# Gathering neighbours on quarters of the matrix array, in sixteen chunks of 64 columns

## The chip, the cores and the metric

The kernel runs on one core of a Trainium2 chip. The core has a matrix engine (TensorE, "PE" in the profile, with its weight loads apart as "PEld"), a vector engine (VectorE, "DVE"), a scalar engine (ScalarE, "ACT"), a general engine (GpSimd, "POOL") and SyncE ("SP"), which here issues all DMAs. Each engine works through its own list in order and waits on semaphores for the others. The metric is the device time of one execution, in microseconds (us); lower is better.

## The reference

Two graph layers over 16 graphs of 1024 nodes with 64 features. About 8 in 1000 entries of the adjacency are set, apart from the diagonal, which is always set. Layer 0 is attention with 8 heads over the neighbours, layer 1 additive attention with one head; each is followed by a residual sum and a layer normalisation.

```python
# layer 0, per graph
scores = einsum('bmhd,bnhd->bhmn', q, k) * scale + edge_bias[edges]
scores = where(edges > 0, leaky_relu(scores, 0.2), -1e9)
x = layernorm(x + einsum('bhmn,bnhd->bmhd', softmax(scores), v) @ Wp + bp)
# layer 1, per graph
e = einsum('bijf,f->bij', leaky_relu(u[:, :, None] + v[:, None], 0.2), a)
e = where(adj > 0, e, -9e15)
x = layernorm(x + elu(einsum('bij,bjf->bif', softmax(e), hp)))
```

## The kernel before

**Lists in place of a dense matrix.** The rows of a graph are taken in groups of eight (128 groups). For each group the kernel lists the columns in which any of the eight rows has a neighbour, and gathers those columns of x once for all eight. A second, dense version (`all_pairs`) stands behind a flag and runs only if some list overflows. A group has 120 slots: two halves of 56 (`CAP2`) and the eight rows themselves.

**Making the lists (`prepare`).** Per graph the adjacency is loaded, reduced with a matmul to one number per group and column (`pat`, L347; how many rows have it and which), and turned into keys (L353) that hold that number and the column. The columns stand in four segments of 256. VectorE takes the largest keys of a segment eight at a time (`max`, L359 and L392) and strikes them out (`match_replace`, L360 and L394), five rounds in all. Between the first and the second round, L367 to L385 split columns that several rows share into one key per row (`MULT` = 4). A segment gives 34 slots (`WIN`); two neighbouring segments share the 12 middle ones of a half, the second filled from its far end (L402, L403). The columns of the slots go to DRAM (`col_d`, L412), the row codes too (`slot_d`, L424), and come back spread over the partitions as `rows_s` (16 DMAs, L431), from which `finish` makes the mask. `prepare` is a generator of 41 pieces.

**Gathering.** 128 rows make 8 tiles of 16 groups. For each tile and layer, `load` (L482) spreads the tile's column list `col_d` over all partitions as `cb`; `indicate` (L494) compares it with the partition's own number, twice (`jrow`, once for each 128 columns of a segment), which gives the 0/1 matrix `f`; `gather` (L518) multiplies x, split exactly into three bf16 parts (`t3`, made by `thirds` on GpSimd), with `f`. Its matmuls contract over all 128 partitions and write 64 of the 128 output partitions each; one half of the slots (`hs`) is 26 matmuls, most with 272 columns, into one PSUM bank, and ScalarE copies it to `xg` (L524).

**Around it.** Layer 0: `queries` (L623) makes q for the tile; `score` (L644) multiplies it with `xg` and adds the mask; VectorE adds a constant (`sc`, L652) and makes the leaky relu and the row maximum (L660, L661); `exps` (ScalarE, L670), `divide` (VectorE's reciprocal L677 and GpSimd's product L678), `turn` and `turn_weights` (transposes L537 and L686), `attend` (L696), `heads` (L712) and `rows` (L728). Layer 1: `own_rows` (L771 on GpSimd), `project` (L779, L785, then relu L791 and sum L792), `weigh` (L806), `exps`, `turn_weights` (L820, copied to `eT` by ScalarE, L822), `attend` (L831), `rows` (L289).

**Order of the work.** All of it is written out by hand, with every engine's list in program order. The main loop makes one step per tile: in step g layer 0 gathers tile g, scores tile g-1 and finishes g-2 and g-3, while layer 1 does the same for tile u = g - 12. So 12 steps have layer 0 alone, 116 both layers and 12 layer 1 alone, and a few close the pipeline. At five places in a step (`lists.place`) pieces of the next graph's `prepare` are put in, by a quota per step (`QUOTA`), and one piece of GpSimd and normalisation work from two side lists.

**Buffers that set an order.** In PSUM, tag "g" has two banks (gather halves, layer 1's transposes, `pa`), "s" two (score, `po`, `pz`), "p" two (queries, transposes), "e" one: `back`, `pe` of `weigh` and `pt1` of layer 1's `turn_weights` take turns in it. In SBUF `cb` has three buffers, `f` four, of which a tile uses two.

## Time and profile before

| What | Value |
|---|---|
| median of 3 runs | 2473.73 us (2468.94 to 2477.21) |
| the profiled execution, span | 2474.2 us |
| TensorE busy | 2230.1 us (90%), 46658 matmuls |
| VectorE busy | 1858.2 us (75%) |
| ScalarE busy | 1602.8 us (65%) |
| GpSimd busy | 1227.3 us (50%) |
| DMA queue of the kernel | 29.7% of 16 engines' span, 231.85 MB |
| first `score` starts, last one | 85.5 us, 2319.7 us |
| one batch (8 steps) in the middle | 144 to 147 us |

A group line reads: line, engine, operation, output<-inputs, size, x how often | busy time in us, mean ns of one | idle time of the engine just before them in us, and what ended most of it. Matmuls are pipelined: the mean of one is from its start to its end, and several are under way at once, so busy time, not count times mean, is what they cost. A timeline line reads: start in us, duration in us, engine, line, operation, and how many were merged into it. A line of busy times by stretch reads: stretch, its length, busy time of each engine with the number of its instructions, the granted share of TensorE's clock, the DMA engines' share and GB/s.

### The profile page before, as it was taken

The page shows a single profiled execution, that of the slowest core. Times are in us where ns is not written, and L with a number is a line of the kernel's source. Part 1 is how long each engine was busy: PE and PEld are TensorE (multiplying, and loading weights), DVE is VectorE, ACT ScalarE, POOL GpSimd, SP SyncE. Part 2 cuts the span into 40 slices and gives each one's busy share as a digit, 9 for nine tenths or more (in the row PEclk, how much of TensorE's full clock was granted, in tenths as well). Part 3 has the DMA queues.
Part 4 walks back from the last instruction along what each step waited for, and adds up shares of the span by engine and source line. Part 5 has one row for each costly group of instructions (what it writes and reads, how often), then busy time and mean ns, then how long its engine had stood idle before and what let it go on. Part 6 is the DMA issues. An engine that isn't in the chain of part 4 may idle for free. (4 is left out here: it accounts for less than half of the span.)

```text
span 2474.2 us, 107346 instructions
## 1 busy us (share of the span) xinstructions
PE 2230.1 (90%) x46658; PEld 1852.8 (75%) x46658; DVE 1858.2 (75%) x4591; ACT 1602.8 (65%) x5585; POOL 1227.3 (50%) x1570
## 2 busy tenths in 40 slices
PE   4577999999999999999999999999999999999995
PEld 3466877777787777778777777787777788788763
DVE  5587888787878878787787878778787877866532
ACT  2255766767677676767667676776767667677753
POOL 1133545545464555546456454545645555555552
PEclk9688999999999999999999999999999999999998
DMA  3422422423333242333224233232423323132110
GB/s 104 133 63 87 134 102 80 142 78 112 110 97 104 74 148 78 117 105 104 97 73 149 78 105 117 91 109 73 150 79 105 103 93 113 58 101 75 52 47 21
DMA packets 192691, 238.78 MB, mean 97 GB/s; under 512 B 91732, under 2 KB 157332, under 8 KB 192212
## 3 DMA queue, kind: packets, MB, share of 16 engines
q1 hardware_dynamic: 192212, 231.85, 29.7%
q8 instruction: 368, 6.03, 1.0%
q14 instruction: 111, 0.91, 0.1%
HBM read 226.58 MB, written 5.21 MB: 94 GB/s over the span
## 5 line engine op out<-in xcount | busy, mean ns | idle before, releaser
L518 PE MATMUL pg<-f,x 128*64 128x272 bf16 (+2 forms) x13312 | 822.5, 276 | 43.5 <-DVE f L494 28.7
L518 PEld LDWEIGHTS <-x 128*64 128x64 bf16 x13312 | 675.0, 111 | 158.6 <-issue 125.8
L678 POOL TENSOR_TENSOR ls<-ls,den 128x480 f32<-128x480 f32 x256 | 294.7, 1151 | 677.7 <-DVE den L677 677.0
L494 DVE TENSOR_SCALAR f<-cb,jrow 128x2176 bf16<-128x2176 bf16 x512 | 457.9, 935 | 11.4 <-DMA cb<-col_d 11.4
L524 ACT COPY xg<-pg 128x448 f32<-128x448 f32 x512 | 267.5, 525 | 299.8 <-PE pg L518 299.8
L670 ACT ACTIVATE ls<-ls,mx 128x120 f32<-128x120 f32 x1024 | 391.0, 386 | 0.0
L537 PE MATMUL pt<-ident,xg 128*120 128x128 f32 x2048 | 276.3, 277 | 34.6 <-DVE qp L628 22.7
L538 ACT COPY xn<-pt 120x512 f32<-120x512 f32 x512 | 277.0, 598 | 30.4 <-PE pt L537 26.8
L537 PEld LDWEIGHTS pt<-ident,xg 128*120 128x120 f32 x2048 | 224.2, 138 | 66.3 <-DVE qp L628 33.5
L771 POOL TENSOR_TENSOR rq<-rw,in_q 128x960 bf16<-128x960 bf16 x128 | 235.8, 1842 | 69.7 <-ACT rw L769 69.6
L791 ACT ACTIVATE r<-pz 128x480 f32<-128x480 f32 x256 | 131.7, 566 | 158.0 <-PE pz L785 158.0
L652 DVE TENSOR_TENSOR sc<-s,rowc 128x480 f32<-128x480 f32 x256 | 155.5, 648 | 88.6 <-PE s L644 88.4
L792 DVE SCALAR_TENSOR_TENSOR r<-pz,r 128x480 f32<-128x480 f32 x256 | 155.2, 648 | 69.6 <-ACT r L791 69.6
L670 ACT ACTIVATION_READ_ACCUMULATOR ls<-ls,mx 128x1 f32 x1024 | 194.6, 190 | 0.0
L688 ACT COPY w<-pp 120x512 f32<-120x512 f32 x256 | 138.1, 590 | 63.2 <-PE pp L686 63.2
L660 DVE SCALAR_TENSOR_TENSOR ls<-sc 128x480 f32<-128x480 f32 x256 | 179.0, 699 | 0.0
L628 DVE TENSOR_TENSOR qp<-pq,qb 128x256 f32<-128x256 f32 x256 | 96.0, 417 | 108.4 <-PE pq L623 108.4
L661 DVE TENSOR_REDUCE mx<-ls 128x4 f32<-128x480 f32 x256 | 167.2, 653 | 8.8
L696 PE MATMUL z<-w,xn 120*64 120x64 f32 x4096 | 155.4, 229 | 5.6 <-ACT w L688 5.6
L503 POOL COPY xg<-xT 128x64 f32<-128x64 f32 x256 | 110.9, 450 | 93.1 <-PE pt L537 93.0
L696 PEld LDWEIGHTS z<-w,xn 120*64 120x64 f32 x4096 | 135.9, 141 | 28.2 <-ACT w L688 27.5
L779 PE MATMUL pz<-xg,w2d 64*64 64x480 f32 x1024 | 143.0, 571 | 13.9 <-DVE sc L652 13.9
(228 smaller groups left out, 4184.1 us busy)
## 6 DMA issues: line engine op xcount, KB each, us to landing
cb<-col_d SPq DMA_DIRECT2D x271, 544.0 KB
ad<-in_adj_dram SPq DMA_DIRECT2D x256, 256.0 KB
xs<-in_x_dram SPq DMA_DIRECT2D x32, 128.0 KB
rows_s<-slot_d SPq DMA_DIRECT2D x256, 14.0 KB
out_dram<-o SPq DMA_DIRECT2D x32, 128.0 KB
col_d<-col SPq DMA_DIRECT2D x128, 4.2 KB
dg<-in_adj_dram SPq DMA_DIRECT2D x32, 2.0 KB
slot_d<-slot SPq DMA_DIRECT2D x16, 28.0 KB
```

What stands on the lines that cost most here:

```text
L494: nc.vector.tensor_scalar(fj.rearrange("p s n q k -> p (s n q k)"), cb.rearrange("p s n q k -> p (s n q k)"), jrow[:, j : j + 1], None, AL ...
L518: nc.tensor.matmul(pg[sub(n), :, FIRST * a_ + lo : FIRST * a_ + to], self.t3[:, k, 4 * hs + 2 * a_ + j, :], f[j][:, 2 * hs + a_, n, :, lo:to],
L524: nc.scalar.copy(dst, pg)
L537: nc.tensor.transpose(pt[:, q, :], xg[:, 4 * m + q, :], ident)
L538: nc.scalar.copy(self.xn[t][:, ts(m, 4), :], pt)
L652: nc.vector.tensor_tensor(sc, both[n], self.rowc[:, n, ts_].unsqueeze(2).to_broadcast([P, 4, SLOTS]), ALU.add)
L660: nc.vector.scalar_tensor_tensor(ls, scs[n], SLOPE, scs[n], ALU.mult, ALU.max)
L661: nc.vector.tensor_reduce(self.mx[:, n, ts_], ls, XX, ALU.max, negate=True)
L670: nc.scalar.activation(ls[:, q, :], ls[:, q, :], AF.Exp, bias=neg[:, q : q + 1], accum_out=den[:, q : q + 1])
L678: nc.gpsimd.tensor_tensor(ls, ls, den.unsqueeze(2).to_broadcast([P, 4, SLOTS]), ALU.mult)
L696: nc.tensor.matmul(zz[sub(n), q, :], xn[:, q, sub(n)], w_[n][:, q // 2, sub(q % 2)], start=True, stop=True)
L771: nc.gpsimd.tensor_tensor(rq, rw.unsqueeze(1).to_broadcast([P, NQ, SLOTS]), in_q.unsqueeze(2).to_broadcast([P, NQ, SLOTS]), ALU.mult)
```

## The change

The columns are taken in 16 chunks of 64 in place of four segments of 256. A chunk has up to 16 entries: the eight largest keys (a first `max`, then one `match_replace`), and a second `max` over the rest and the extra keys of shared columns, of which only the first four keys of a chunk are now split. A half of the slots now serves eight chunks; chunk T gets a window of 18 slots that starts at `STARTS[T]`, so that neighbouring windows overlap by 12 or more. Where a chunk needs more than its own gap, the rest shifts into its neighbour's: a running sum (`tensor_tensor_scan`) gives each chunk's shift, and five predicated copies move the keys by 16, 1, 2, 4 and 8 places as its bits say; `put` is filled by GpSimd. The slot list is the maximum over the eight overlapping windows.

Each chunk's 64 columns stand on 64 partitions, two chunks above each other, so that one `indicate` makes the whole `f` (2304 columns, three buffers). `gather` writes both halves in one go: 96 matmuls with 64 contracted partitions, 64 output partitions and 144 columns, four of them on the four quarters of the array, into two banks. The column list `cb` comes in two DMAs of 64 partitions each, `rows_s` in one. In the main loop each layer has one gather in place of two, `queries` stands ahead of both `rows`, the exponentials of layer 0's second half stand together, a second `load(0)` of the next graph is gone, the pieces are 38 and the quotas fit them.

```diff
-WIN = 34
+CH = 64
+WIN = 18
+STARTS = (0, 4, 10, 16, 22, 28, 34, 38)
...
-            for s in range(2 * hs, 2 * hs + 2):
-                nc.vector.max(lst[:, s, 0:8], ka[:, s, 0:SEG])
-                nc.vector.match_replace(kb[:, s, 0:SEG], lst[:, s, 0:8], ka[:, s, 0:SEG], -1.0)
+            for T in range(c, c + 4):
+                for n in range(2):
+                    nc.vector.max(lst[:, 0, T, n, :], ka[:, T, n, :])
+                    nc.vector.match_replace(kb[:, T, n, 0:CH], lst[:, 0, T, n, :], ka[:, T, n, :], -1.0)
                 yield
...
+        for T in range(NT):
+            for n in range(2):
+                nc.vector.max(lst[:, 1, T, n, :], kb[:, T, n, :])
...
+        nc.gpsimd.memset(ends[:, :, 0:1], 0.0)
+        nc.vector.tensor_tensor(free, cnt[:, 0], gap, ALU.subtract)
+        nc.vector.tensor_tensor(free, free, cnt[:, 1], ALU.add)
+        for n in range(2):
+            nc.vector.tensor_tensor_scan(ends[:, n, 1 : NT + 1], nought, free[:, n, :], 0.0, ALU.max, ALU.add)
...
+        put = per.tile([P, 4 * NT, PAD + WIN], F32, tag="ka", name=f"put_{b}")
+        nc.gpsimd.memset(put, 0.0)
+        for r in range(2):
+            nc.gpsimd.tensor_copy(
+                put[:, 2 * NT * r : 2 * NT * r + 2 * NT, PAD : PAD + 8].rearrange("p (n t) k -> p n t k", n=2),
+                lst[:, r].rearrange("p t n k -> p n t k"),
+            )
+        yield
+        wide = 8
+        for k in (4, 0, 1, 2, 3):
+            wide = WIN if k == 4 else min(wide + (1 << k), WIN)
+            low = PAD - (1 << k)
+            nc.vector.copy_predicated(
+                put[:, :, PAD + wide - 1 : PAD - 1 : -1],
+                bit[:, k, :].unsqueeze(2).to_broadcast([P, 4 * NT, wide]),
+                put[:, :, low + wide - 1 : (low - 1 if low else None) : -1],
+            )
...
+        nc.gpsimd.memset(slot, 0.0)
+        for T in range(NT):
+            at_ = slot[:, :, STARTS[T] : STARTS[T] + WIN]
+            nc.vector.tensor_tensor(at_, at_, who[:, :, T, :], ALU.max)
...
+            self.cb[t] = cb = dbl.tile([P, 2, NQ, NT, WIN], BF16, tag="cb", bufs=3, name=f"cb_{nm}")
+            for n in range(2):
+                nc.sync.dma_start(
+                    cb[sub(n)].rearrange("p n q t k -> p (n q t k)"),
+                    edges[self.b][t, n].rearrange("n q k -> (n q k)").unsqueeze(0).to_broadcast([D, 2 * NQ * NT * WIN]),
+                )
...
+            self.f[t] = f = dbl.tile([P, 2, NQ, NT, WIN], BF16, tag="f", bufs=3, name=f"f_{nm}")
+            nc.vector.tensor_scalar(
+                f.rearrange("p n q t k -> p (n q t k)"), cb.rearrange("p n q t k -> p (n q t k)"),
+                jrow, None, ALU.is_equal,
+            )
...
-        def gather(self, t, hs):
+        def gather(self, t):
+            pg = [ps_g.tile([P, NQ, CAP2], F32, tag="g", name=f"pg_{nm}_{c}") for c in range(2)]
+            f = self.f.pop(t)
+            for T, at_ in enumerate(STARTS):
+                for k in range(3):
+                    for c, n in CORNERS:
+                        nc.tensor.matmul(
+                            pg[c][sub(n), :, at_ : at_ + WIN], self.t3[sub(c), k, T, :], f[sub(c), n, :, T, :],
+                            start=(T + k == 0), stop=(T == NT - 1 and k == 2), skip_group_check=True,
+                        )
+            for c in range(2):
+                nc.scalar.copy(self.xg[t][:, :, c * CAP2 : c * CAP2 + CAP2], pg[c])
...
-            at(l0, g - 2, "exps", 1, range(2))
-            at(l0, g, "gather", 0)
+            at(l0, g, "gather")
             at(l0, g - 3, "heads")
-            at(l0, g, "gather", 1)
-            at(l0, g - 2, "exps", 1, range(2, 4))
+            at(l0, g - 2, "exps", 1, range(4))
+            at(l0, g, "queries")
             at(l1, u - 3, "rows", back)
             at(l0, g - 3, "rows", back)
-            at(l0, g, "queries")
...
-            at(l1, u, "gather", 0)
+            at(l1, u, "gather")
             at(l0, g - 1, "turn")
             at(l1, u - 2, "turn_weights")
...
-            at(l1, u, "gather", 1)
             at(l1, u - 1, "weigh")
```

## The prediction

> **What bounds the kernel now.** I read the page's first part and the costliest groups first, then the busy time of the engines in one batch (eight steps) of the steady part and in the last six steps of layer 0, where no batch is prepared any more, then the groups of TensorE and VectorE by shape, and last the timeline around layer 1's gather.
>
> ```profile
> span 2474.2 us, 107346 instructions
> ...
> PE 2230.1 (90%) x46658; PEld 1852.8 (75%) x46658; DVE 1858.2 (75%) x4591; ACT 1602.8 (65%) x5585; POOL 1227.3 (50%) x1570
> ...
> L518 PE MATMUL pg<-f,x 128*64 128x272 bf16 (+2 forms) x13312 | 822.5, 276 | 43.5 <-DVE f L494 28.7
> ```
> ```profile
> core 0: us, PE busy (x) PEld busy (x) DVE busy (x) ACT busy (x) POOL busy (x), PEclk, DMA share, GB/s
> 1123.70:1270.50 146.80, 136.83 (x2910) 114.26 (x2908) 115.89 (x281) 99.07 (x348) 77.02 (x98) 0.98 0.32 102
> ...
> 2208.20:2304.70 96.50, 95.58 (x2094) 81.25 (x2092) 60.70 (x124) 71.21 (x238) 47.80 (x57) 1.00 0.23 75
> ```
> TensorE is busy 137 of 147 us in a batch that prepares its successor and 95.6 of 96.5 without; VectorE is next (116), then ScalarE (99). The gather, L518, is over a third of TensorE. So the bound is TensorE's stream, with VectorE 20 us a batch behind it.
>
> ```profile
> L644 PE MATMUL s<-mask,rep_q 64*64 64x120 bf16 x2048 | 51.6, 215 | 2.4 <-issue 2.4
> ```
> ```profile
> L494 DVE TENSOR_SCALAR f<-cb,jrow 128x2176 bf16<-128x2176 bf16 x512 | 457.9, 935 | 11.4 <-DMA cb<-col_d 11.4
> ...
> L392 DVE MAX8 lst<-kb 128x8 f32<-128x280 f32 x128 | 56.8, 443 | 0.0
> ...
> L359 DVE MAX8 lst<-ka 128x8 f32<-128x256 f32 x64 | 26.9, 420 | 0.6
> ```
> The two timelines, TensorE's and ScalarE's, of one step:
> ```profile
> 2230.77 1.58 PE L518 MATMUL pg<-f,x 128*64 128x272 bf16 x26
> 2232.29 1.09 PE L537 MATMUL pt<-ident,xg 128*120 128x128 f32 x8
> 2233.21 0.27 PE L820 MATMUL pt<-ident,e 128*120 128x128 f32 x1
> 2233.41 1.59 PE L518 MATMUL pg<-f,x 128*64 128x272 bf16 x26
> 2234.93 0.62 PE L806 MATMUL e<-r,a_two 128*32 128x120 f32 x16
> ```
> ```profile
> 2232.43 0.51 ACT L524 COPY xg<-pg 128x448 f32<-128x448 f32 x1
> 2232.98 1.07 ACT L538 COPY xn<-pt 120x512 f32<-120x512 f32 x2
> 2233.93 0.28 ACT L822 COPY eT<-pt 120x128 f32<-120x128 f32 x1
> ```
> These show what the second half of layer 1's gather does now besides gathering: it fills TensorE from 2233.41 to 2234.93 while ScalarE turns out xg, xn and eT. L806 writes the one PSUM buffer "e" that eT is copied from, so it may not start before that copy ends.
>
> **The change, part by part.**
>
> *Gather on quarters.* A half is 26 matmuls from 2230.77 to 2232.29, 1.52 us, two per pass (a pass is one tile of one layer): 3.04. After it, 96 matmuls of 144 columns in 24 fours. The nearest row is L644 with the mask: quarters of 64x64, bf16, new weights each, rows and banks crossed in the same way. 128 groups of 16: 51.6/128 = 0.403 us, less one duration of 0.215, is 0.188 us for 15 starts, 12.5 ns each, 50 ns a four of 120 columns. 144 columns make 60 ns, 24 fours 1.44, with the first weights 1.5 us. It saves 1.54 a pass, 3.08 a step with both layers, 394 us over 256 passes if TensorE sets the time throughout. Ends: 72 ns a four if fixed cost per instruction rises (1.8 a pass), 1.44 below.
>
> Against this stands a rule of the Trainium skill, "TensorE: Matmul & The Clock Gate", section "Wait — 56ns, not 53.3ns?": starts are never closer than about 25 ns, however small the matmul. An estimate from that page makes a pass 96 x 25 = 2.4 us and the step's saving 1.28, which the wait below would eat: no gain. The row says 12.5 ns between different quarters, so I go by the row.
>
> *Both halves at once: a new wait.* Layer 1's order becomes gather, turn (L537), turn of weights (L820), weigh (L806), with no second half between the last two. Cover left: L537 and L820, 2232.29 to 2233.41, 1.12 us. ScalarE in that time has now two xg copies, then xn, then eT: it starts 0.14 after the gather, two copies some 0.5 apart make 1.0, xn to eT's start 0.95, eT 0.28: 2.4 us. L806 waits 1.3 us in each of 128 steps; what is queued behind it on TensorE (turn of layer 0's weights, L696, L831, the next score) moves by as much. Bounds: 0 where TensorE had to wait just before anyway, 2.1 where the normalisation's four small ScalarE operations (some 0.2 each) stand in front. I take 1.3, as the chain is ScalarE's own and nothing shortens it.
>
> *Less slack elsewhere.* From score to L537 of layer 0 TensorE loses 1.5 us of work, in which VectorE does sc, ls, mx and qp (some 5 us) and, when preparing, a piece of about 1 us first. L537 and L779 will wait more often for VectorE. Heads stays one gather behind the score, as now. Moving queries ahead of rows covers the copy of aT (two of 363 ns) with 0.55 us in place of 1.52: 0.2 in odd steps. Together 0.2 a step; ends -0.5 (VectorE is relieved, below) and +1.0 (a whole piece).
>
> *VectorE.* One indicator of 2304 in place of two of 2176: 1.87 becomes 0.935 x 2304/2176 = 0.99, -0.88 a pass, -14 us a batch. Preparing: MAX8 falls from 443 at 280 and 420 at 256 by about 0.9 ns an element, to 0.25 us at 64; MATCH_REPLACE (434 and 409) to 0.21, its value load stays 0.09. Now 20 x 0.44 + 16 x 0.52 = 17.1 us; then 32 x 0.25 + 16 x 0.30 = 12.8. Added: some 22 small operations of about 0.2 (4.4), five predicated copies of together 2272 elements, which no row shows (at 1.36 ns an element, L660's pace over 480, 3.1; twice that above, half below), wider list operations (1.5); the integer subtraction L380 (510 ns) turns into a float one near 0.19 (-1.3). Net +3.4 a batch (-1 to +9), so VectorE falls from 116 to about 105 us a batch. It stays beside TensorE's work.
>
> *POOL, SP, DMAs.* POOL gets the memset of put, two copies, two small memsets: some 2.3 us a batch against 77 busy of 147; put is issued one place ahead of its readers. If POOL is late at ends or slot, VectorE waits up to one L771 (1.84 us), inside the +1.0. On SP, rows_s goes from 16 issues to 1, col_d from 8 to 4, cb from 1 to 2 per pass, the doubled load(0) goes: about three fewer issues a batch, and bytes of cb up 6% at a DMA share of 0.32. Nothing, covered by a step of lead; without it a cb load shows as VectorE's wait (11.4 us in the whole run now, at the start). At the start the longer list work (+3.4) and four column-list issues saved (SP's timeline has the eight at 65.72 for 5.05 us, 0.63 each) cancel within 2 us.
>
> *Instructions.* TensorE gets 24% more. Its stalls without a cause (the timeline has one of 1.15 us inside a gather at 1035.35) come about once per batch, 1.2 to 2 us; four more make +6.
>
> *Sum.* 116 steps with both layers: -3.08 + 1.3 + 0.2 = -1.58, -183 us. 12 steps of layer 0 alone, with VectorE busy 143 of the 180 us from 100 on and TensorE no fuller: -0.7 each, -8. 12 of layer 1 alone: -1.54 + 1.3, -3. Stalls +6. Together -188: 2474.2 becomes 2286. The profiled span is 0.5 us from the median of the three runs, 2473.73, so it needs no correction.
>
> A second rule bears on the waits: the same page, section "What's actually happening", says that TensorE drops to half clock after an idle window of about 3.4 us. This trace shows it in one step a batch:
>
> ```profile
> 1536.60:1560.00 23.40, 20.26 (x427) 16.84 (x425) 19.46 (x45) 12.39 (x42) 13.45 (x16) 0.93 0.45 129
> ```
> There L712 waits 3.00 us for VectorE and the next two groups run slow (2.36 and 2.50 us for 1.10 and 1.59). New waits of 1.3 us stay below such a window; by the rule nothing changes while no wait doubles.
>
> **Rivals.**
> *No new wait shows (12%).* If TensorE's waits only swap places, 116 x 3.08 + 24 x 1 - 6 = 375 off: 2100 to 2180 us. For it: ScalarE has 25% idle time. Against: eT's chain is serial.
> *VectorE and ScalarE take over (13%).* With 2.1 for eT and 1.0 for VectorE the step gains nothing: 2460; half-way 2370. For it: after the change TensorE's own work is some 112 us a batch against VectorE's 105 and ScalarE's 99, three engines in fixed order. This case holds what chance there is for no change.
> *The quarters don't overlap (6%), the slower side.* If row quarters that add into the same columns run one after the other, a four takes 120 ns, a pass 2.9 us, and the wait of 1.5 stays: 116 x 1.2 more, 2620 us. It decides from 95 ns a four on (2.29 us a pass). For it: runs of 18 elements, 288 bytes apart, that no row shows on quarters. Against: L644, and L785 with three additions in place.
> *The change does not do what it says (1%).* If a list overflowed, the all-pairs part would run and add thousands of us. Counting the reference's adjacency: the fullest window takes 17 of 18 slots, a chunk has at most 3 shared columns of 4, and 6 late entries of 7.
>
> **How the numbers follow.** The forecast (68%) spans 2200 to 2360: 1.58 a step with 0.7 either way. The range 2140 to 2400 leaves out the lower half of the first rival, the upper third of the second and the last two, 0.2. Faster by over 0.3% (7 us, about what a measurement can tell): 0.68 + 0.12 + 0.11 = 0.91; within 0.02; slower 0.07.
>
> **What would show it.** The gather: L518's successor in quarters, about 1.5 us between a pass's first matmul and the next group, 12 to 16 ns a start. The wait: "PE e <- ACT eT" among TensorE's waits with 100 to 170 us, now 12. VectorE near 1700 us busy, f 256 times at about 1 us. A batch near 132 us, TensorE at 85 to 90% of it. Wrong: eT's wait under 50 us, or a new first releaser (qp, sc, a copy predicated in front of sc), or fours above 75 ns.

## The result, and the profile after

The change made the kernel slower: 2557.26 us, median of 4 runs (2544.11 to 2563.3), against 2475.47 us for the kernel before; the ratio is 1.0317, with a 95% interval of 1.0279 to 1.0356. Forecast were 2286 us (2140 to 2400). The profiled execution of the changed kernel spans 2553.1 us at a granted clock of 0.924; before, 2474.2 at 0.964.

The first part of the page, the groups of the gather and of layer 1's first projection matmul, and the row of instruction packets, all of the kernel after:

```profile
span 2553.1 us, 130753 instructions
...
PE 1972.4 (77%) x57922; PEld 1670.9 (65%) x57922; DVE 1828.5 (72%) x5009; ACT 1584.6 (62%) x5585; POOL 1182.1 (46%) x1667
...
q8 instruction: 456, 7.47, 1.3%
```
```profile
L574 PE MATMUL pg<-f,x 64*64 64x144 bf16 x24576 | 485.7, 228 | 177.4 <-issue 98.3 <-DVE u L814 37.4 <-DVE f L554 32.7
...
L832 PE MATMUL pz<-xg,w2d 64*64 64x480 f32 x1024 | 158.3, 667 | 3.7 <-issue 2.3 <-DVE sc L705 1.0 <-PE back L781 0.4
```

The gather did become cheap: 822.5 us fell to 485.7. The sum that closes is this. TensorE's gather lost 336.8 us. The rest of its busy time, with the same instructions as before, rose from 1407.6 to 1486.7, by 79.1; L832, for instance, took 143.0 before. The time in which TensorE does nothing (span less busy) rose from 244.1 to 580.7, by 336.6. Together +78.9, which is the difference of the spans. So the whole gain of the gather was given back as idle time, and slower work elsewhere came on top.

What the idle time is made of is in TensorE's waits (what, for whom: us in total, times, longest). After:

```profile
PE e L859 <- ACT eT L875: 161.7, 124, 2.9
PE pg L574 <- issue: 98.3, 65, 5.2
PE po L765 <- DVE sc L705: 60.6, 17, 5.3
PE pq L676 <- issue: 38.6, 24, 3.1
PE pg L574 <- DVE u L814: 37.4, 14, 3.7
```
Before:
```profile
PE po L712 <- DVE sc L652: 45.3, 14, 4.7
PE pg L518 <- DVE f L494: 28.7, 1, 28.7
PE pt L537 <- DVE qp L628: 22.7, 22, 5.4
PE pz L779 <- DVE sc L652: 13.9, 15, 1.0
PE e L806 <- ACT eT L822: 13.2, 15, 0.9
```

Three things are new: the wait for eT, which was forecast; the wait for u; and "issue", a pause in which TensorE waits for no engine and no transfer that the profile shows. From here on I count such a pause only where neither the matmuls nor the weight loads run for over 50 ns and the next instruction has no releaser, and call it a *stall without a cause*. So counted there were 28 before (63 us, of which 29 at the start) and 142 after (223 us). The timeline shows one, in the middle of a gather (start, duration, operation, in brackets the idle time before it):

```profile
1256.03 1.61 PE L574 MATMUL pg<-f,x 64*64 64x144 bf16 x91
1260.64 0.44 PE L574 MATMUL pg<-f,x 64*64 64x144 bf16 x5 [3.00 <-issue]
...
1264.41 1.88 PE L832 MATMUL pz<-xg,w2d 64*64 64x480 f32 x8
...
1282.21 1.03 PE L832 MATMUL pz<-xg,w2d 64*64 64x480 f32 x8
```
91 of 96 matmuls ran, then nothing for 3 us, then the last five. The same lines show the second loss: 4 us after the stall L832 takes 1.88 us for what takes 1.03 one step later. The granted clock of that stretch (after the length come PE, PEld, DVE, ACT and POOL, then the clock, the DMA share and GB/s):

```profile
1257.64:1270.00 12.36, 9.05 (x206) 6.93 (x206) 6.02 (x19) 5.97 (x22) 2.68 (x3) 0.72 0.15 35
1290.00:1320.00 30.00, 26.32 (x868) 23.35 (x868) 26.70 (x76) 20.13 (x73) 16.64 (x23) 0.94 0.51 126
```
In the clock records of these two traces the granted clock is either full or a half: a half for 389 us of the span after and 177 before, with TensorE busy for 307 and 114 us of it. L832 takes nearly twice as long in such a stretch. An estimate from these numbers: about half of the 193 us more, some 97 us of TensorE's time in the gather and in the rest, went to the clock.

Where the stalls without a cause fall is regular. Numbered along TensorE's own stream (matmuls and weight loads), neighbouring stalls are mostly 256, 509, 764 or 1020 instructions apart; 120 of the 141 distances lie within 8 of a multiple of 255. Queue q8 brings 456 packets of 7.47 MB together, 16 KB each, and between the starts of two packets TensorE starts 246 instructions (median). A stall ends 1.42 us (median) after the end of the latest packet; before, 1.48. Of the stalls after, 91% end 1.0 to 1.8 us behind a packet; of moments taken at random, 15% lie there. So I read the stalls as TensorE standing still because a block of some 255 of its instructions has not arrived. A block ahead of a stall, the stall included, took some 4.5 us (median), the fastest 2.8. The gather uses 192 instructions in 1.5 us, with 96 of the score in front of it (1.2 us) and 64 each of heads (1.0) and queries (0.5) behind. Before, half a gather was 52 instructions in 1.5 us.

The theory to test: the time is set by *late instructions*, and columns no longer count. The rivals: the *waits* for eT and u; *VectorE*, whose list work grew; and the *clock*.

### The profile page after: what moved, and what is told of

It reads as the page before. It is cut to its first block, busy times and chain, and to the rows that moved or that the text cites. A ratio compares the mean times of both kernels' runs of the same rounds, so it can differ in the third digit from the quotient of the medians.

```text
span 2553.1 us, 130753 instructions
## 1 busy us (share of the span) xinstructions
PE 1972.4 (77%) x57922; PEld 1670.9 (65%) x57922; DVE 1828.5 (72%) x5009; ACT 1584.6 (62%) x5585; POOL 1182.1 (46%) x1667
## 3 DMA queue, kind: packets, MB, share of 16 engines
q8 instruction: 456, 7.47, 1.3%
## 4 chain that ended last, share of the span: by engine, by line
PE 45%; DVE 26%; ACT 14%; issue 10%; POOL 2%; DMA 2%; SPq 1%; POOLq 0%; DVEq 0%; ACTq 0%
PE pg L574 8%; PE pz L832 4%; PE s L697 4%; PE po L765 4%; ACT xn L591 4%; ACT xg L579 3%; PE pp L739 3%; PE z L749 3%; PE pt L590 3%; DVE put L456 3%; PE pz L838 3%; PE e L859 3%; ACT r L844 3%; DVE f L554 3%; PE pq L676 3%
## 5 line engine op out<-in xcount | busy, mean ns | idle before, releaser
L574 PE MATMUL pg<-f,x 64*64 64x144 bf16 x24576 | 485.7, 228 | 177.4 <-issue 98.3
L574 PEld LDWEIGHTS <-x 64*64 64x64 bf16 x24576 | 440.4, 109 | 215.8 <-issue 195.9
L579 ACT COPY xg<-pg 128x448 f32<-128x448 f32 x512 | 246.3, 532 | 370.4 <-PE pg L574 370.1
L824 POOL TENSOR_TENSOR rq<-rw,in_q 128x960 bf16<-128x960 bf16 x128 | 230.9, 1804 | 88.4 <-ACT rw L822 88.4
L590 PEld LDWEIGHTS pt<-ident,xg 128*120 128x120 f32 x2048 | 235.7, 142 | 32.4 <-DVE qp L681 17.8
L554 DVE TENSOR_SCALAR f<-cb,jrow 128x2304 bf16<-128x2304 bf16 x256 | 219.0, 855 | 7.1 <-DMA cb<-col_d 7.1
L859 PE MATMUL e<-r,a_two 128*32 128x120 f32 x2048 | 81.7, 279 | 166.0 <-ACT eT L875 161.7
L713 DVE SCALAR_TENSOR_TENSOR ls<-sc 128x480 f32<-128x480 f32 x256 | 189.2, 739 | 0.0
L859 PEld LDWEIGHTS e<-r,a_two 128*32 128x32 f32 x2048 | 47.7, 111 | 196.3 <-ACT eT L875 195.6
L765 PE MATMUL po<-zT,wvp 64*64 64x128 f32 x2048 | 109.5, 342 | 78.6 <-DVE sc L705 60.6
L832 PE MATMUL pz<-xg,w2d 64*64 64x480 f32 x1024 | 158.3, 667 | 3.7 <-issue 2.3
```

Of the source, the lines that this page charges most:

```text
L554: nc.vector.tensor_scalar(f.rearrange("p n q t k -> p (n q t k)"), cb.rearrange("p n q t k -> p (n q t k)"), jrow, None, ALU.is_equal,)
L574: nc.tensor.matmul(pg[c][sub(n), :, at_ : at_ + WIN], self.t3[sub(c), k, T, :], f[sub(c), n, :, T, :], start=(T + k == 0), stop=(T == NT - ...
L579: nc.scalar.copy(self.xg[t][:, :, c * CAP2 : c * CAP2 + CAP2], pg[c])
L590: nc.tensor.transpose(pt[:, q, :], xg[:, 4 * m + q, :], ident)
L765: nc.tensor.matmul(po[n][sub(c_), :], wvp[sub(n), 2 * h + c_, :], self.zT[sub(n), 2 * h + c_, :, :, :].rearrange("p o q i -> p (o q i)"), ...
L824: nc.gpsimd.tensor_tensor(rq, rw.unsqueeze(1).to_broadcast([P, NQ, SLOTS]), in_q.unsqueeze(2).to_broadcast([P, NQ, SLOTS]), ALU.mult)
```

## The experiments

All times are medians of several rounds. The kernel before lay between 2474.65 and 2478.98 us in these comparisons. The last three columns are from each profiled execution; "other gaps" are all other gaps over 50 ns of TensorE, waits for engines and transfers.

| Kernel | us | ratio to before (95%) | TensorE busy | stalls without a cause | other gaps |
|---|---|---|---|---|---|
| before | 2475 | 1 | 2230 | 63 | 154 |
| after | 2557 | 1.0279 to 1.0356 | 1972 | 223 | 331 |
| e1 weights first | 2528 | 1.0170 to 1.0248 | 2000 | 240 | 261 |
| e2 half columns | 2566 | 1.0334 to 1.0430 | 1898 | 269 | 363 |
| e3 before, split | 2516 | 1.0132 to 1.0215 | 2257 | 101 | 131 |
| e4 two parts | 2499 | 1.0055 to 1.0109 | 1874 | 182 | 417 |
| e5 e1 + u elsewhere | 2517 | 1.0153 to 1.0258 | 2006 | 246 | 236 |
| e6 e5, no shift | 2461 | 0.9890 to 0.9970 | 1982 | 247 | 205 |
| e8 e5, spread order | 2552 | 1.0293 to 1.0348 | 2049 | 139 | 330 |
| e9 e5, loads twice | 2554 | 1.0296 to 1.0396 | 2008 | 306 | 210 |
| e10 e5, even lists | 2521 | 1.0143 to 1.0213 | 2021 | 183 | 288 |
| e11 e5, queries later | 2575 | 1.0374 to 1.0450 | 2064 | 182 | 292 |
| e12 e10 + e11 | 2543 | 1.0219 to 1.0302 | 2054 | 144 | 322 |
| e13 e12, heads later | 2669 | 1.0738 to 1.0814 | 2151 | 125 | 374 |
| e14 e5, half of ab on ScalarE | 2492 | 1.0027 to 1.0065 | 1982 | 220 | 267 |
| e15 e5, most of ab on ScalarE | 2492 | 1.0032 to 1.0065 | 1998 | 196 | 274 |
| e16 e6, no lists | 2444 | 0.9835 to 0.9868 | 1986 | 233 | 200 |
| e17 before, no lists | 2383 | 0.9602 to 0.9634 | 2187 | 61 | 99 |
| e18 e16, two parts | 2374 | 0.9567 to 0.9639 | 1859 | 166 | 303 |
| e19 e16, queries later | 2478 | 0.9969 to 1.0026 | 2022 | 181 | 247 |

**Waits, columns, density, number (e1 to e4).** e1 takes the cover of eT from layer 0's transposes: layer 1's weights are turned ahead of them.

```diff
             at(l1, u, "gather")
-            at(l0, g - 1, "turn")
             at(l1, u - 2, "turn_weights")
+            at(l0, g - 1, "turn")
```


> The changed kernel with layer 1's turn of weights (the transpose copied to eT) put ahead of layer 0's turn, nothing else. Theory: TensorE's waits and its starved instruction stream add up on one path. ScalarE then copies eT right after the two xg copies, so the weighing's wait for eT falls from 162 us to under 50, and the time by 80 to 140, to 2415 to 2480 us. Rival: VectorE and ScalarE have become the bound, TensorE's waits only show it; then the wait moves to another place and the time falls by less than 30.

The wait fell as intended (TensorE's waits of e1):

```profile
PE pg L574 <- issue: 99.5, 67, 5.5
...
PE pg L574 <- DVE u L814: 50.3, 14, 4.4
...
PE e L859 <- ACT eT L875: 40.1, 26, 2.2
```
122 us of wait less bought 29 us: far under the 80 to 140 of the theory, at the edge of the rival's 30. The waits for u and the stalls without a cause grew by 13 and 17 us, and TensorE's busy time by 28.

```diff
+                        h = WIN // 2 if k else WIN
-                            pg[c][sub(n), :, at_ : at_ + WIN], self.t3[sub(c), k, T, :], f[sub(c), n, :, T, :],
+                            pg[c][sub(n), :, at_ : at_ + h], self.t3[sub(c), k, T, :], f[sub(c), n, :, T, 0:h],
```


> The changed kernel in which the second and third part of x are gathered for only the first 9 of each window's 18 slots: the same 96 matmuls and weight loads a pass, two thirds of the columns (the gathered values are wrong in the other slots). Instruction theory: TensorE runs out of instructions about every 255 of them, so a pass that is 0.5 us shorter starves 0.5 us more; the 223 us without a releaser grow by 60 or more, and the time falls by 0 to 60 from 2557 us. Rival, the array's pace: 256 x 0.5 = 128 us faster, 2430.

```profile
L575 PE MATMUL pg<-f,x 64*64 64x72 bf16 (+1 forms) x24576 | 386.5, 214 | 209.4 <-issue 122.4 <-DVE u L815 40.6 <-DVE f L554 35.3
```
The gather's busy time fell by 99 us and nothing came of it (2566 us, no better than after). Its stalls without a cause rose by 46 us (60 or more were forecast), the other gaps by 32. So the gather's columns do not count any more; their number is not what can be saved.

e3 leaves the gather of the kernel before as it was in work and cuts each matmul in two.

```diff
-                            for n in range(2):
+                            for qs in (slice(0, 4), slice(4, 8)):
+                                for n in range(2):
...
-                                    pg[sub(n), :, FIRST * a_ + lo : FIRST * a_ + to],
+                                        pg[sub(n), qs, FIRST * a_ + lo : FIRST * a_ + to],
...
```


> The kernel before with each gather matmul cut in two along its columns (four groups each): 13312 more matmuls and as many loads, the same columns, some 2.5 ns more each (33 us). If the number of instructions is what counts, TensorE's idle time without a releaser grows from 63 to 200 or more and the time by 130 to 190 us over 2475; if it is how dense they come (68 per us here, 120 in the changed gather), it stays under 130 and the time grows by 30 to 100. Rival, instructions cost nothing: under 35 us.

```profile
L519 PE MATMUL pg<-f,x 128*64 128x136 bf16 (+2 forms) x26624 | 856.7, 223 | 62.6 <-issue 30.4 <-DVE f L494 29.7 <-ACT xg L526 2.0
```
e3 issues more matmuls than the changed kernel (59970 against 57922) and lost 39 us, with 38 us more of stalls. A stream with more instructions costs, then, but the number alone gives at most a quarter of the changed kernel's new stalls (+38 against +160). As forecast for the case that density counts, the stalls stay under 130 us: e3 uses 104 instructions in the time in which the changed gather uses 192.

```diff
-                for k in range(3):
+                for k in range(2):
...
```


> The changed kernel with the third part of x left out of the gather (the values lose their last bits): 64 matmuls a pass in place of 96, and the same columns as with the halved windows of the run before. Instruction theory: 16384 fewer TensorE instructions; idle time without a releaser falls from 223 to 120 or less, and it is 80 us or more faster than the halved windows, 2330 to 2430. Rival, the array's pace: the same as the halved windows within 25 us.

8192 matmuls and as many weight loads fewer took 58 us off the changed kernel, and 66 off e2, which has as many columns: less than the 80 that late instructions alone had to give, more than the rival's 25. The stalls fell by 42 us from after, to 182 and not to the 120 or less of the theory, and the wait for eT grew, from 165 to 195 us counted as gaps.

**Order and traffic (e5, e8, e9).** e5 is e1 with the sums of the source rows in other banks; all later versions build on it.

```diff
-            pu = ps_g.tile([P, NT, D], F32, tag="g", name=f"pu_{self.b}")
+            pu = ps_z.tile([P, NT, D], F32, tag="z", name=f"pu_{self.b}")
```


> The weights-first version with the sums of the source rows (pu, eight a batch) moved from the gather's banks to the ps_z pool, so that a gather no longer waits for VectorE to copy them out; nothing else changes. In the weights-first version TensorE waits 50 us for that copy. If this wait lies on the path, it goes: 2480 to 2500 us against 2528.2, and the waits for u fall under 10 us. If TensorE is then only stopped by late instructions sooner, their stalls (240 us there) grow by 20 to 40 us and the time falls by under 20 us.

The wait for u is gone. The median fell by 11 us, but against the kernel before e1 stands at 1.0209 and e5 at 1.0206, so a gain is not shown. The stalls rose by 7 us, not by the 20 to 40 that late instructions were to add. e1 and e5 together removed 159 us of these two waits and got 40 us (27 by the ratios).

e8 puts the step's dense parts apart:

```diff
+            at(l0, g - 2, "exps", 1, range(2))
+            at(l0, g - 1, "turn")
             at(l0, g, "gather")
             at(l0, g - 3, "heads")
-            at(l0, g - 2, "exps", 1, range(4))
-            at(l0, g, "queries")
+            at(l0, g - 2, "exps", 1, range(2, 4))
             at(l1, u - 3, "rows", back)
+            at(l0, g - 2, "divide", 1)
+            at(l1, u - 1, "project")
...
-            at(l0, g - 2, "divide", 1)
-            at(l1, u - 1, "project")
...
-            at(l0, g - 1, "turn")
...
+            at(l0, g - 2, "turn_weights")
             at(l1, u - 1, "weigh")
...
-            at(l0, g - 2, "turn_weights")
             at(l1, u - 1, "turn")
             at(l1, u - 1, "exps")
+            at(l0, g, "queries")
```


> The kernel of the sums elsewhere with the same instructions of TensorE in another order of the step: the score is followed by the transposes of layer 1, layer 0's gather comes before heads, then the projection, and the queries are moved behind layer 1's transposes and exponentials; so the short-lived instructions (gather, heads, queries) no longer stand one behind the other. If the stalls for instructions come from dense stretches in a row, they fall by 50 to 120 us and the time with them, to 2380 to 2460 us, under the kernel before. If they come from the number of instructions in all, they stay within 30 us of the kernel of the sums elsewhere; what the time then does is the new order's own waits.

The stalls fell by 107 us, inside the forecast, and the time rose by 36 us. In their place stand (waits of e8):

```profile
PE pg L574 <- ACT xg L579: 53.2, 28, 3.8
PE e L859 <- ACT eT L875: 50.2, 69, 1.8
PE pt L873 <- DVE o L898: 49.4, 52, 2.4
PE po L765 <- DVE sc L705: 36.1, 25, 2.8
PE pg L574 <- issue: 34.4, 37, 2.4
```
So the stalls do follow the density of the stream, but shorter stalls did not make a shorter step.

e9 doubles the traffic of the column loads:

```diff
-            for n in range(2):
+            for n in (0, 1, 0, 1):
                 nc.sync.dma_start(
                     cb[sub(n)].rearrange("p n q t k -> p (n q t k)"),
```


> The kernel of the sums elsewhere with each load of the slots' numbers (cb) issued twice into the same tile: the traffic of that queue goes from 35% of the DMA engines' time to some 65%, TensorE's and VectorE's work stays the same. If the instruction packets come late because they share the DMA engines with these loads, a packet takes longer than 1.12 us, the stalls for instructions grow by 80 us or more and the time by as much. If the supply has its own pace of some 3.5 us for 255 instructions, stalls and time stay within 15 us.

The load queue of e9, then of e5:

```profile
q1 hardware_dynamic: 214372, 383.54, 56.6%
```
```profile
q1 hardware_dynamic: 173412, 232.51, 36.1%
```
The traffic went from 36.1% of the engines' time in e5 to 56.6%, the stalls from 154 of together 246 us to 185 of 306 us, the time up 37 us. Neither forecast held: with more traffic there are more stalls, hardly longer ones (1.60 and 1.65 us each), and the mean time of an instruction packet barely moved (1.13 to 1.16 us), so where the instructions wait stays open.

**VectorE's lists (e6, e10).** e6 leaves out the shift for all batches but the first.

```diff
+            if b == 0:
             nc.vector.copy_predicated(
```


> The kernel of the sums elsewhere without the five predicated copies for every batch but the first: the slots that neighbours share stay where the rank puts them, so the gathered values are not the reference's, and all sizes, transfers and TensorE instructions are the same. These copies take 86.6 us of VectorE in the changed kernel, some 75 of them left out here. If VectorE's lists hold the long step of each batch, the time falls by 50 to 90 us against the kernel of the sums elsewhere. If they lie beside TensorE's late instructions, by under 20 us.

56 us (68 by the ratios) for 57 us of VectorE's busy time, with the stalls where they were (247). This is the only change of one thing that brought its full price. One step in each batch holds the end of the list work. The timeline of the kernel after shows one, VectorE's lines first, then TensorE's:

```profile
1322.21 5.69 DVE L456 COPY_PREDICATED put<-bit,put 128x576 f32<-128x576 int32 x5
1327.79 0.80 DVE L554 TENSOR_SCALAR f<-cb,jrow 128x2304 bf16<-128x2304 bf16 x1
...
1329.87 1.78 DVE L473 TENSOR_SCALAR win<-win 128x288 int32<-128x288 int32 x1
...
1333.14 1.80 DVE L486 TENSOR_TENSOR slot<-slot,who 128x36 bf16<-128x36 bf16 x8
1334.86 1.22 DVE L705 TENSOR_TENSOR sc<-s,rowc 128x480 f32<-128x480 f32 x2
```
```profile
1328.32 0.39 PE L697 MATMUL s<-mask,rep_q 64*64 64x120 bf16 x16
...
1335.57 2.33 PE L765 MATMUL po<-zT,wvp 64*64 64x128 f32 x29 [3.68 <-DVE sc L705]
```
The score is done at 1328.7, but VectorE, behind the copies, works on two indicators and pieces of `prepare` until 1334.9. sc comes 6 us after the score, and TensorE waits 3.68 us.

> The kernel of the sums elsewhere with the pieces of a batch's list work spread more evenly over its eight steps: 4, 5, 5, 5, 5, 5, 5, 4 in place of 3, 3, 5, 5, 5, 5, 6, 6. In that kernel the step with the last pieces takes 23 to 25 us, with 18 us of VectorE and two waits of TensorE for it (3.7 us for sc, 1.9 for eT). Leaving out the copies took 56 us off. If it was this long step that cost, evening it out brings 40 to 80 us: 2440 to 2480 us, no slower than the kernel before. If it was VectorE's sum over the batch, under 20 us.

```diff
-    QUOTA = (3, 3, 5, 5, 5, 5, 6, 6)
+    QUOTA = (4, 5, 5, 5, 5, 5, 5, 4)
```
No gain (+4 us by the medians, within the noise): the earlier pieces ran ahead of the adjacency they read. VectorE waited 148.0 us for it, against 40.1 in e5 (VectorE's waits, of e10 first, then of e5). TensorE's wait of L832 for sc, 0.7 us in e5, came to 84.3 in e10 (last line):

```profile
DVE ab L345 <- DMA ad<-in_adj_dram: 148.0, 74, 6.0
```
```profile
DVE ab L345 <- DMA ad<-in_adj_dram: 40.1, 33, 3.6
```
```profile
PE pz L832 <- DVE sc L705: 84.3, 32, 6.4
```

**Later queries, later heads (e11 to e13).**

```diff
-            at(l0, g, "queries")
...
             at(l1, u - 1, "exps")
+            at(l0, g, "queries")
```


> The kernel of the sums elsewhere with layer 0's queries moved from behind heads to behind layer 1's exponentials, the one move of the spread order that does not touch a gather. There TensorE waits 47 us for instructions at the queries. If a dense stretch cut short lowers the stalls, they fall by 30 to 60 us in all, and as no wait for another engine is added the time falls by 20 to 50 us. If the stalls only move to the next place, under 15 us. If the queries' result comes too late for the score (sc through qp), waits for qp above 15 us appear and the time does not fall.

65 us of stalls less, 59 us slower. The waits of e11 show what took their place; qp, which was named, is one of four:

```profile
PE pg L574 <- ACT xg L579: 31.4, 28, 2.1
PE pz L832 <- DVE sc L705: 31.2, 26, 2.6
...
PE s L697 <- DVE qp L681: 23.1, 18, 3.0
PE pp L739 <- ACT xn L591: 17.3, 10, 2.4
```


> Even lists and later queries together. If the two costs are apart, the gains add: 2400 to 2450 us, 1 to 3% under the kernel before. If both were slack of the same path, it is within 15 us of the better of the two.

The gains did not add, as there were none: e12 lies between e10 and e11. e13 moves `heads` and its rows behind `project`:

```diff
-            at(l0, g - 3, "heads")
...
             at(l1, u - 1, "project")
+            at(l0, g - 3, "heads")
+            at(l0, g - 3, "rows", back)
+            at(l0, g - 3, "residual")
...
```


> Even lists and later queries, and heads with its rows moved behind layer 1's projection, so that layer 0's gather is no longer followed by heads (192 instructions in 1.6 us, then 64 in 1.0). By dense stretches the stalls for instructions fall by another 20 to 50 us and the time with them. If the spread order was slow because of late results and not because of its gathers, new waits appear here too, for what heads and rows feed, and the time does not fall.

The fewest stalls of all orders (125 us), and the slowest kernel: TensorE waits 112.9 us for r in front of L765 (`heads`), the granted clock is 0.890, and TensorE is busy 2151 us.

```profile
PE po L765 <- DVE r L845: 112.9, 59, 3.1
```

**How much VectorE counts, in both kernels (e14 to e19).** e14 and e15 compute everything; they move a half and three quarters of the adjacency's conversion.

```diff
-                if b:
+                if b and T % 2:
                     nc.vector.tensor_scalar(ab[:, T, :, :], ad, 1.0 - TINY, 0.0, ALU.subtract, ALU.max)
```


> The kernel of the sums elsewhere with every second adjacency tile turned into bf16 (ab, 462 ns on VectorE) by ScalarE's Relu instead, the form that the first batch has (718 ns): VectorE loses some 55 us, ScalarE gains some 86. If VectorE's work is what the time now follows (leaving the copies out took 57 us off VectorE and 56 off the time), it falls by 30 to 60 us, to 2455 to 2485 us. If only the place of the copies mattered, or ScalarE's results are late instead, under 20 us.

> The same with three of four of these tiles on ScalarE: VectorE loses some 83 us, ScalarE gains some 130 (1579 to 1710 us busy). If the time follows VectorE alone, 55 to 90 us under the kernel of the sums elsewhere: 2425 to 2460 us, faster than the kernel before. If ScalarE is as near to the path as VectorE, it is slower than with half of them.

25 us each by the medians and 39 by the ratios to the kernel before (one of e5's four runs lies 21 us above the next). So whether e14 reached the 30 to 60 us of the theory that the time follows VectorE is not settled; e15 is under its 55 to 90 either way. VectorE's busy time fell by 48 and 76 us, ScalarE's rose by 65 and 102; the second step brought nothing, and a wait of L357 for ScalarE's zT grew from 6.1 us in e5 to 22.1 and 38.1. Of the versions that compute everything e14 and e15 are the fastest built on the change, and still 0.3 to 0.7% over the kernel before.

```diff
+                    if b == 0:
                         nc.vector.max(lst[:, 0, T, n, :], ka[:, T, n, :])
                         nc.vector.match_replace(kb[:, T, n, 0:CH], lst[:, 0, T, n, :], ka[:, T, n, :], -1.0)
...
+                if b == 0:
                     nc.vector.max(lst[:, 1, T, n, :], kb[:, T, n, :])
```


> The kernel without the copies, and for every batch but the first also without the searches for the largest eight (L372, L373 and L407: 190 us of VectorE); the lists are then empty and the gathered values wrong, with all sizes, transfers and TensorE instructions as they were. If the time follows VectorE, it falls by 110 to 180 us more, to 2280 to 2350 us. If the late instructions hold it now that the long step is gone, it stays within 40 us of 2461.

> The control: the kernel before, for every batch but the first without the seven later rounds of its search (L392 and L394, some 195 us of VectorE); values wrong in the same sense, all else as it was. If the kernel before is bound by TensorE alone, it stays within 20 us of its 2476 us. If VectorE's work lies on its path too, it falls by 60 us or more, and then VectorE's share is nothing that the change brought.

In both the second of the two forecasts came. The busy times of e16 and e17:

```profile
PE 1985.7 (81%) x57922; PEld 1668.3 (68%) x57922; DVE 1604.9 (66%) x3974; ACT 1576.7 (64%) x5585; POOL 1178.2 (48%) x1697
```
```profile
PE 2187.2 (92%) x46658; PEld 1823.5 (77%) x46658; DVE 1667.0 (70%) x3991; ACT 1605.0 (68%) x5585; POOL 1227.8 (52%) x1585
```
In the changed kernel 145 us less of VectorE, after the copies, took only 17 us off, while 191 us less took 96 off the kernel before (2478.98 in that comparison). VectorE's lists lay on the path of the kernel before too; the wait of po for sc (45.3 us) is gone in e17, and the clock rose to 0.977. With the lists gone from both, the kernel with the changed gather is 61 us slower, with 172 us more of stalls without a cause (233 against 61) and 100 us more of other gaps, against 201 us less of TensorE's busy time.

> The kernel without the lists, and without the third bf16 part in the gather (8192 instructions of TensorE fewer, some 100 us of its busy time; values wrong as there). If TensorE with its late instructions is what is left on the path, the stalls fall from 233 to some 150 us and the time by 100 to 180 us, to 2265 to 2345 us. If the loop is held by the other engines' results in turn, whatever TensorE does, it falls by under 50 us.

71 us off for 8192 matmuls and their loads, between the two forecasts: in the profiled execution (16 us under the median) stalls -67, TensorE's busy time -127, the other gaps +103. TensorE's stream counts there, but some half of what it gives up is filled by results that are not ready.

> The kernel without the lists, with layer 0's queries moved behind layer 1's exponentials. The same move made the kernel of the sums elsewhere 59 us slower although its stalls for instructions fell by 65. If that was because VectorE was close behind, the fall of the stalls shows in the time here: 30 to 65 us under 2444. If the late queries cost by themselves (the score waits for qp, the gather for xg), it is slower than 2444 here too.

Slower by 33 us also without the lists: the late queries cost by themselves. From the waits of e19:

```profile
PE pg L580 <- ACT xg L585: 31.9, 28, 2.1
```
The wait of the gather for xg is the one of e11 (31.4), and it stays without the lists; that of the score for qp (23.1 there) falls to 4.6.

**What is settled.** The gather's gain ended as idle time of TensorE. Removal gives these prices: the waits for eT and u 40 us together (27 by the ratios), the copies 56 (68), the columns nothing, the third part of the gather (8192 matmuls and their loads) 58 to 71. The two waits and the copies alone make 96 us, more than the loss of 82: without them, at 2461 us, the kernel is 14 us under the one before, but its shifted slots are wrong. The stalls without a cause are the largest single part of the new idle time (160 of 337 us, with 148 for eT), and they follow the density of TensorE's instructions (e3, e8). What they cost by themselves is not settled; that they kept the rest of the gain from coming is likely (e2, e4, e18) and argued, not shown: no run removed them without moving or taking away work, and each reordered version turned them into waits. Nor does any run set the clock alone; that TensorE's other work took 79 us longer is read from the trace, and the 97 us above are an estimate.

## Why the prediction was wrong

*What bounds the kernel.* "The bound is TensorE's stream, with VectorE 20 us a batch behind it" was half right. e17 shows 96 us of the kernel before hanging on VectorE's lists. Busy time over a batch hid that about one step in eight waits for them (14 waits for sc, 45.3 us).

*Gather on quarters.* Right. The chain of waits of the kernel after (start, duration, piece) has the 96 matmuls of one pass, from its first start to the next group's:

```profile
1241.18 1.50 PE pg L574 x96
```
1.50 us, as forecast, is 15.6 ns a start. The row (12.5 ns for 120 columns, 15 for 144) stood against the rule of the Trainium skill ("TensorE: Matmul & The Clock Gate", section "Wait — 56ns, not 53.3ns?", 25 ns a start), and the measurement sides with the row: the rule does not hold across quarters here. The rival "quarters don't overlap" fell with it. But this is a pass at full clock without a stall: over all 256 passes the group is busy for 485.7 us, 1.90 us each, so TensorE's gather lost 337 us in place of the 384 that the sum took.

*The new wait.* Right in place and size: 161.7 us for 124 waits, 1.3 us each, with 166 forecast. Its price was wrong: e1 took 122 us of it away for 29. Summed up as if each wait lengthened the step, it was counted at several times its worth; in a step with several waits in turn, the next one takes the place of the one removed.

*VectorE.* The indicator fell as forecast (219.0 us in all, 0.86 us each, 0.99 forecast), and the searches too (10.8 us a batch, 12.8 forecast). The rest of the preparation was mis-sized. VectorE's busy time without the indicator rose by (1828.5 - 219.0) - (1858.2 - 457.9) = 209 us, 13.1 a batch where +3.4 stood (bounds -1 to +9). The copies measured 5.4 us a batch for the 3.1 taken (their upper bound was 6.2; the 1.36 ns an element is L661's pace, not L660's, which is 1.46), and small operations took more than 0.2 us: L473 1.65, L384 1.55, L427 1.03. The timelines show why: a small list operation that begins beside a GpSimd operation often lasts until that one ends. L384, a cast of 64 elements, in the kernel after, and what GpSimd does then:

```profile
371.80 1.79 DVE L384 CAST ki<-lst 128x64 int32<-128x64 f32 x1
```
```profile
371.69 1.84 POOL L824 TENSOR_TENSOR rq<-rw,in_q 128x960 bf16<-128x960 bf16 x1 [0.80 <-ACT rw L822]
```
The same two engines in e5:

```profile
372.87 0.61 DVE L384 CAST ki<-lst 128x64 int32<-128x64 f32 x1
```
```profile
372.78 0.65 POOL L528 CAST x<-y 128x512 bf16<-128x512 f32 x1
```
Where GpSimd is idle, L384 takes 0.19 us. In the kernel after, all 41 runs of L384, L385 and L394 that began while a GpSimd operation had longer to go than they need ended within 0.15 us of its end; of the second search (L407) only 3 of 99 did. If each form of the preparation's operations is taken at its shortest duration, the preparation is 521 us before and 597 after, 4.7 a batch more, near the +3.4. The time above the shortest rose from 83 to 221 us, and 211 of the 221 lie in operations that ran beside one of GpSimd. So what failed in this term is mostly the time that VectorE's small operations lose beside GpSimd, which the sum had at nothing. VectorE ended at 1828.5 us, not 1700. "It stays beside TensorE's work" failed: e6 prices the copies at 56 us.

*POOL, SP, DMAs.* The wait of VectorE for cb was 7.1 us in all, 11.4 before: the loads cost nothing there, as said. That more of them goes with more stalls of TensorE (e9) was not thought of.

*Instructions.* This is the term that failed by the most. "TensorE gets 24% more. Its stalls without a cause come about once per batch, 1.2 to 2 us; four more make +6." They rose from 28 to 142, by 160 us. The step counted instructions and scaled a rare event by hand, four more of them in all; the stalls go with how many the stream needs in 3 to 4 us (e3, e8), and the changed gather, with the score ahead of it, needs 288 in 2.7 us. A look at where the few stalls before stood could have told it: they end 1.48 us after a packet, and 17 of their 27 distances lie within 8 of a multiple of 255.

In TensorE's own time the forecast can be set against the result term by term. The sum took 384 us off for the gather (116 x 3.08, 12 x 0.7 and 12 x 1.54) and put on 190 for waits (116 x 1.5 and 12 x 1.3) and 6 for stalls: -188. The traces show 337 off, 177 more of other gaps, 160 more of stalls, and 79 more for the rest of TensorE's work, which the sum had at nothing: +79. So the waits came out in sum about as forecast, and of the 267 us between forecast and result 154 are stalls, 79 the slower rest and 47 the gather's smaller gain, less 13 of waits. This says where the time lies; what it would bring to remove the stalls alone stays open, as no run does that.

*The clock.* The rule that the clock halves after an idle window ("What's actually happening", same page, about 3.4 us) was set aside as "new waits of 1.3 us stay below such a window". The stalls were longer: gaps of TensorE over 2 us, between 100 and 2400 us of the span, went from 20 to 81. In the same stretch the granted clock fell to a half 20 times before and 74 times after, and 71 of the 74 have a gap of over 2 us within the 6.8 us ahead. Only 30 gaps are over 3.0 us, so shorter ones than the page's figure stand ahead of a half clock here too. In the row above a stall of 3.00 us opens a stretch at a clock of 0.72, and the mean fell from 0.964 to 0.924.

*Rivals.* None came as drawn. "VectorE and ScalarE take over" (2460 at its worst) had the mechanism of the waits but ended at no gain. None of the rivals had the supply of instructions, and the one slower case was about the array's pace, which held.

## What to carry to other kernels

Before many short matmuls replace few long ones, divide the instructions of the densest few microseconds by what the trace has shown the engine to get: here about 255 TensorE instructions, weight loads among them, in some 3.5 us (half of the 7.1 that two blocks ahead of a stall took at the least). A pause inside one uninterrupted group, with no releaser and a packet of the instruction queue just before its end, is the sign. And do not add up waits: in a loop in which several engines take turns, price each by removing it (29 us for 122, nothing clear for 50, but 56 for 57), because only what lies on the path all along pays in full. And price a small VectorE operation with what GpSimd does beside it: here 0.19 us became 1.79.

## What the runs showed of the hardware

- TensorE stalls where a block of instructions is late. The points are mostly multiples of some 255 instructions apart, the packets are of 16 KB, and a stall ends 1.42 us after the packet's end. Two blocks in a row ahead of a stall never took under 7.1 us in the changed kernel and 6.2 in e2, some 72 and 82 instructions a us.
- More traffic of loads goes with more of these stalls: 154 (246 us) became 185 (306 us) when the load queue went from 36.1% to 56.6% of the DMA engines' time.
- Four quarters of the array with 64 contracted rows, 64 outputs and 144 columns start 15.6 ns apart, and half of the columns in two thirds of them saved TensorE 99 us of the gather's busy time and no time in all.
- Some small VectorE operations lasted until the GpSimd operation beside them ended: the cast of 64 elements of L384 took 0.19 us with GpSimd idle, 0.61 beside a cast (L528) and 1.79 beside a product (L824), with the same code. The eight-largest search of L407 mostly did not (3 of 99).
- The granted clock was either full or a half in these traces, a half for 177 us before and 389 after.
